# Taking the segment sum's product ahead of the bias products in a graph-network kernel

## Chip, cores and metric

The kernel runs on one core of a Trainium2 chip. Its engines are TensorE (PE in the profile, its weight loads PEld), VectorE (DVE), ScalarE (ACT), GpSimd (POOL) and SyncE (SP). Each takes its own instructions in order; they wait for each other through semaphores, called signals here. The metric is the time of one execution in microseconds of the device (us).

## What is computed

One layer of message passing over a graph of 12,500 nodes and 200,000 edges, all sizes 64 per side. `ssp` is softplus minus log 2. Cut to its core:

```python
nodes = node_state[edges].reshape(num_edges, -1)          # rows of source and target, side by side
gates = ssp(edge_state @ We1 + be1) @ We2 + be2
soft_cutoff = 1.0 - jax.nn.sigmoid(5.0 * (edges_distance - (CUTOFF - 1.5)))
gates = gates * soft_cutoff
h = ssp(nodes @ Wn1 + bn1) @ Wn2 + bn2
messages = h * gates
message_sum = jnp.zeros_like(node_state).at[edges[:, 1]].add(messages)
new_state = node_state + (ssp(message_sum @ Ws1 + bs1) @ Ws2 + bs2)
```

The result is the layer norm of `x + new_state`. The edges are sorted by their target node.

## The kernel before

The edges are cut into 391 groups of 512, and the main loop (from L688) has one step for each group. Step i does the first layers of group i+1, the second layers and the message of group i, and the sum of group i-2. The order is written out by hand: the order of the calls in the loop is the order on each engine. Because the edges are sorted, a half group of 256 edges reaches a window of 42 neighbouring nodes, and its sum is a product of its messages with a 0/1 matrix (the one-hot).

TensorE's instructions of a usual step, in order, each with its line:

- `layer1_bias`, L296: the edge layer's bias into the z tile of group i+1 (three rows of bfloat16, 256 columns).
- `layer2_bias`, L347: the second layers' biases into the gh tile of group i (three rows of bfloat16, 512 columns).
- `scatter`, L376: the product of messages and one-hot of group i-2, two matmuls in float32. It writes 84 columns in the second half of the new z tile, where room is left. From twelve steps before the end on (`CLOSE`) it takes the messages of group i-1, those of the step just before. In the first of these steps it takes both.
- `transposes`, L283: the four gathered tiles of group i+1, into the tx tile.
- `layer1_edge`, L301, then a filler, L334 (in the first steps L646, a part of a table), then `layer1_node`, L308, which waits for ScalarE's copy of the transposes, L291.
- a filler, L334, and `layer2`, L354 and L359, which wait for VectorE's L330. Where a node block is due, its products follow: L415, or L443 and L446.

A float32 matmul of the program is two passes in the profile (a transpose is one), so that L376 counts four a step, L359 eight, L354, L308 and L283 four.

ScalarE copies the transposes (L291), copies single columns (L259), and takes exponential and logarithm of the z tile (L322, L325). VectorE multiplies the second layer's result with the cutoff (L368, which waits for L359) and makes the message (L372), then the softplus (L330) and the one-hot (L277), and adds the sums' product to the running sums (L396, after the logarithms).

GpSimd issues the gathers, L204: four indirect DMAs a group, of 128 rows of x each. Some groups have three, where one tile comes by single columns instead. The gathered tiles `xg` have eight buffers, and the last reader of one is the group's `scatter`. So GpSimd may run ahead until it meets a buffer whose `scatter` has not been done, and waits there. SyncE issues the loads (L216, L224), which wait for a `scatter` as well.

The z tile has two buffers of two banks, gh and tx have two buffers of one bank.

Of the kernel before, what the change touches and what calls it, by code (L numbers as in the profile page):

```python
# [27 lines left out]
HE = 256  # L28
GE = 2 * HE
W = 42  # L30
# [25 lines left out]
def node_blocks(N):  # L56

    first = N % NB
    assert N > NB and first % 2 == 0 and first <= HE
    sizes = ([first] if first else []) + [NB] * (N // NB)  # L60
    return [(sum(sizes[:i]), n) for i, n in enumerate(sizes)]


def block_steps(N, NG):

    steps = []
    for at, n in node_blocks(N):
        share = sqrt(min(1.0, (at + n) / N))
        spread = sqrt(share * (1.0 - share) / (NG * GE))
        steps.append(ceil(NG * (share + SPREADS * spread)))  # L70
    return steps
# [33 lines left out]
def gnn_resnorm_kernel(ctx: ExitStack, tc: tile.TileContext, a: dict, out: bass.AP, E: int):  # L105
# [24 lines left out]
    def z_tile():  # L130
        return psum.tile([P, 2, NB], F32, name="z")
# [46 lines left out]
    def note(key, ins):  # L178
        made.setdefault(key, []).append(ins)
        return ins  # L180

    def behind(ins, *keys):

        for key in keys:
            for other in made.get(key, []):
                tc.add_manual_dep(ins.ins, other.ins.name,
                                  mybir.DependencyInfo(mybir.DependencyClass.Sync, mybir.DependencyReason.DATA),
                                  reason="one place of a step takes its waits")
# [85 lines left out]
    xTs, zs, us, ss, ghs, hs, msgs, scs = ({} for _ in range(8))  # L274

    def onehot(g):
        last = nc.vector.tensor_tensor(xgs[g][:, :, D:DW], iota, rel[:, g, :].to_broadcast([P, K, W]), OP.is_equal)  # L277
        note(("onehot", g), last)

    def transposes(g, *needs):  # L280
        tx = tx_tile()[:DW].rearrange("f (k e) -> f k e", k=K)
        for k in range(K):
            ins = nc.tensor.transpose(tx[:, k, :], xgs[g][:, k, :DW], ident)  # L283
            if k == 0:
                behind(ins, *needs)
        note(("transposes", g), ins)
        xTs[g] = tx
# [4 lines left out]
        xTs[g] = xT.rearrange("f (t h) e -> f h t e", h=2)  # L292

    def layer1_bias(g, *needs):
        zs[g] = z_tile()
        first = nc.tensor.matmul(zs[g][:, 0, :HE], be3.rearrange("q h d -> q (h d)"), ones3, start=True, stop=False,  # L296
                                 skip_group_check=True)
        behind(first, *needs)
# [75 lines left out]
    def scatter(g, sc):  # L374
        for t in range(2):
            ins = nc.tensor.matmul(sc, msgs[g][:, 2 * t : 2 * t + 2, :].rearrange("p h f -> p (h f)"),  # L376
                                   xgs[g][:, 2 * t : 2 * t + 2, D:DW], start=t == 0, stop=t == 1, skip_group_check=True)
        note(("scatter", g), ins)
        scs[g] = sc
# [106 lines left out]
    with tc.manual_schedule():  # L486
# [50 lines left out]
        def clear(first, last):  # L537
            nc.vector.memset(sums[:, first * P : WIDE if last == NCH else last * P], 0.0)
# [43 lines left out]
        for i, w in enumerate((we2[:D, 0, :], wn2)):  # L582
            n = w.shape[0]
# [83 lines left out]
        with tc.tile_pool(name="finish", bufs=1) as finish:  # L667
            blocks = list(zip(node_blocks(N), block_steps(N, NG)))
            last = NG - 1
            parts, begun, complete, rest = {}, None, 0, []  # L670

            def at(f, g, *more):
                if 0 <= g < NG:
                    f(g, *more)

            def behind_by(i):
                close = last - CLOSE
                return [g for g in ([i - 2] if i <= close else []) + ([i - 1] if i >= close else []) if g >= 0]

            for g in range(LOADS - 1):  # L680
                load(g)
            for g in range(2):
                onehot(g)
            lowest(1, NR)
            everywhere(1, NR)
            clear(0, CHUNKS)
            highest()
            for i in range(-1, last - 1):  # L688
                now = parts.pop(i, [])
                early = [part for part in now if part.tensor]  # L690
                at(load, i + LOADS)
                if i >= 0:
                    at(gather, i + AHEAD, range(K), [("transposes", i)] if i < BEHIND else ())
                layer1_bias(i + 1)
                at(layer2_bias, i)
                for n, g in enumerate(behind_by(i)):
                    scatter(g, zs[i + 1][:, 1, HE + 2 * n * W : HE + 2 * (n + 1) * W])
                transposes(i + 1, ("load", i + 1), ("gather", i + 1), ("onehot", i + 1))
                xcopy(i + 1)
                columns(i, 1, finish)  # L700
                layer1_edge(i + 1)
                c = chunk_of(i, NCH)
                if c is None:
                    busy_before_node(i + 1)
                else:
                    beside_sums = zs[i + 1][:, 1, HE + 2 * W : HE + 2 * W + P]
                    chunk(c, beside_sums)
                layer1_node(i + 1)
                exps(i + 1)
                logs(i + 1)  # L710
                if c is not None:
                    keep_chunk(c, beside_sums)
                read_columns(i + 1, 1)
                for g in behind_by(i):
                    window(g)
                if c is not None:
                    clear(c, c + 1)
                at(busy_before_layer2, i)
                at(layer2, i)
                for part in early:  # L720
                    part.tensor(tx_tile())
                at(hcut, i)
                at(message, i)
                softplus(i + 1)
                for part in early:
                    part.others()
                at(onehot, i + 3)
                read_columns(i, 0)
                columns(i, 0, finish)
                choose(finish)  # L730
                for part in now:
                    if not part.tensor:
                        part.others()
                for action in beside.get(i, []):
                    action()
                complete = i
                if blocks and complete >= blocks[0][1] - PREPARE and not begun:
                    begun = node_block(*blocks[0][0], finish)
                    begun.pop(0).others()
                if blocks and complete >= blocks[0][1]:  # L740
                    steps = next(steps for steps in BLOCK_STEPS if i + steps[-1] < last - 1)
                    for n, part in zip(steps, begun):
                        parts.setdefault(i + n, []).append(part)
                    rest = begun[len(steps) :]
                    blocks.pop(0)
                    begun = None
            assert len(blocks) == 1 and begun and not parts


            begun.pop(2).others()  # L750
            transposes(last, ("load", last), ("gather", last), ("onehot", last))
            xcopy(last)
            layer1_bias(last)
            layer2_bias(last - 1)
            scatter(last - 2, zs[last][:, 1, HE : HE + 2 * W])
            layer1_edge(last)
            layer1_node(last)
            for some in (edge, node):
                exps(last, some)
                logs(last, some)  # L760
            square, variance, root, scale, store = (part.others for part in rest)
            square()
            window(last - 2)
            for g in range(last - 1, last + 1):
                if g not in window_at:
                    window_bases(g)
            layer2(last - 1)
            layer2_bias(last)
            softplus(last, edge)
            layer2_edge(last)  # L770
            softplus(last, node)
            layer2_node(last)
            hcut(last - 1)
            message(last - 1)
            scatter(last - 1, tx_tile()[:, : 2 * W])
            variance()
            root()
            hcut(last)
            message(last)
            scatter(last, tx_tile()[:, : 2 * W])  # L780
            window(last - 1)
            window(last)
            hidden, clamp = begun.pop(0)
            hidden(gh_tile())
            scale()
            clamp()
            store()
            for part in begun:
                node_part(part)
# [162 lines left out]
```

## Time and profile before

| | us |
|---|---|
| three runs | 2393.62, 2394.47, 2402.24 |
| median | 2394.47 |
| the profiled execution, timed | 2389.88 |
| its span, first to last instruction | 2388.1 |

The mean granted clock of TensorE was 0.981 of full speed. How to read what the prediction quotes:

- The page's second line has the busy time of each engine, its share of the span, and its instructions.
- A group's row has line, engine, operation, tiles (out<-in) and count, then busy time and mean ns of one, then the idle time of the engine just before them and what ended most of it.
- A row of the list of waits is: who waited, for whom, us in total, times, longest.
- A row of the order of time is: start in us from the span's start, duration, engine, line, operation, tiles, shape, how many rows are merged, and in brackets the idle time of the engine before and who ended it.
- The name behind the arrow is inferred: it is the last instruction on that engine that had ended when the signal came, which need not be the one that was waited for.

### The profile page before, as it was taken

What the parts mean: (1) busy time and instruction counts of PE and PEld (TensorE: products, weight loads), DVE (VectorE), ACT (ScalarE), POOL (GpSimd) and SP (SyncE); (2) the same over time, 40 slices, a digit from 0 to 9 for tenths busy, and PEclk for the clock granted to TensorE, in tenths of its full rate; (3) what the DMA queues carried; (4) which work ended last, traced back from release to release, by engine and by line L of the source; (5) the groups of instructions that cost most, each with busy time, mean ns of one, the idle gap of its engine ahead of it and who ended that gap; (6) DMA issues with size and microseconds to landing.
All of it is one profiled execution on the core that took longest, in us unless ns stands there. A gap on an engine that the chain in (4) does not pass through costs nothing.

```text
span 2388.1 us, 48209 instructions
## 1 busy us (share of the span) xinstructions
PE 1970.5 (83%) x12897; PEld 1656.7 (69%) x12897; DVE 1293.9 (54%) x5966; ACT 1511.2 (63%) x7412; POOL 1417.0 (59%) x1497
## 2 busy tenths in 40 slices
PE   6788888888888888888888888888888888888877
PEld 4666677767776776677677667766777767777765
DVE  4355555555555555555555555555555555555544
ACT  3466666666666666666666666666666666666653
POOL 5665665666666666666666666665665666666650
PEclk9799999999999999999999999999999999999988
DMA  6332232322222222222222222222222222222220
GB/s 185 85 91 68 56 75 56 77 61 71 54 57 56 53 59 54 57 56 62 53 59 55 57 58 55 59 59 54 58 58 56 59 57 60 63 57 58 59 50 14
DMA packets 159679, 148.63 MB, mean 62 GB/s; under 512 B 40564, under 2 KB 108949, under 8 KB 159274
## 3 DMA queue, kind: packets, MB, share of 16 engines
q1 hardware_dynamic: 111194, 94.97, 14.4%
q0 software_dynamic: 47776, 49.02, 10.8%
q8 instruction: 109, 1.79, 0.3%
q14 instruction: 166, 1.36, 0.2%
q10 hardware_dynamic: 434, 1.50, 0.2%
HBM read 135.70 MB, written 9.62 MB: 61 GB/s over the span
## 4 chain that ended last, share of the span: by engine, by line
PE 80%; issue 13%; ACT 3%; DVE 2%; another core or an unknown queue 1%; DMA 0%; DVEq 0%; ACTq 0%
PE z L308 18%; PE gh L359 13%; PE z L376 10%; PE tx L283 10%; PE gh L354 7%; PE z L301 6%; PE gh L334 4%; PE gh L347 3%; PE z L296 3%; PE z L334 2%; ACT xT L291 2%; PE tx L415 1%; PE tx L446 1%; PE z L311 1%
## 5 line engine op out<-in xcount | busy, mean ns | idle before, releaser
L204 POOL DMA_INDIRECT xg<-in_x,src_i x1493 | 1416.8, 949 | 919.3 <-PE tx L283 488.8
L308 PE MATMUL z<-xT,wns 106*128 106x256 f32 x1564 | 459.7, 412 | 359.9 <-issue 285.9
L291 ACT COPY xT<-tx 106x512 f32<-106x512 f32 x391 | 229.1, 586 | 779.3 <-PE tx L283 751.1
L259 ACT COPY column<-xh 128x4 uint8 x6016 | 608.7, 193 | 0.0
L308 PEld LDWEIGHTS z<-xT,wns 106*128 106x128 f32 x1564 | 267.8, 193 | 452.4 <-issue 337.7
L368 DVE TENSOR_TENSOR h<-gh,cut 128x256 f32<-128x256 f32 x391 | 165.9, 424 | 747.9 <-PE tx L283 632.2
L359 PE MATMUL gh<-consts,s 128*128 128x64 f32 x3128 | 396.0, 270 | 0.0
L359 PEld LDWEIGHTS gh<-consts,s 128*128 128x128 f32 x3128 | 385.0, 194 | 0.1
L325 ACT ACTIVATE u<-u,one 128x768 f32<-128x768 f32 x392 | 365.8, 933 | 13.4 <-ACT u L322 0.5
L330 DVE SCALAR_TENSOR_TENSOR s<-u,z 128x768 f32<-128x768 f32 x392 | 368.7, 941 | 0.4 <-issue 0.4
L322 ACT ACTIVATE u<-z 128x768 f32<-128x768 f32 x392 | 314.7, 803 | 43.4 <-PE z L308 19.0
L396 DVE TENSOR_TENSOR sums<-sums,z 64x42 f32 x778 | 152.4, 196 | 291.3 <-issue 207.4
L376 PEld LDWEIGHTS z<-xg,msg 128*128 128x128 f32 x1556 | 205.0, 192 | 140.6 <-issue 121.3
L376 PE MATMUL z<-xg,msg 128*128 128x84 f32 x1556 | 265.1, 293 | 15.3 <-DVE msg L372 15.3
L259 DVE COPY column<-xh 128x4 uint8 x2944 | 246.5, 219 | 0.4 <-issue 0.4
L354 PE MATMUL gh<-consts,s 128*128 128x128 f32 x1564 | 243.3, 279 | 1.3 <-DVE s L330 0.8
L283 PE MATMUL tx<-consts,xg 128*106 128x128 f32 x1564 | 238.1, 276 | 0.0
L301 PE MATMUL z<-eT,consts 128*128 128x256 f32 x782 | 237.3, 386 | 0.0
L354 PEld LDWEIGHTS gh<-consts,s 128*128 128x128 f32 x1564 | 210.0, 195 | 2.0 <-DVE s L330 1.1
L283 PEld LDWEIGHTS tx<-consts,xg 128*106 128x106 f32 x1564 | 182.5, 142 | 0.9 <-issue 0.9
L372 DVE TENSOR_TENSOR msg<-gh,h 128x256 f32<-128x256 f32 x391 | 165.8, 424 | 13.4
L334 PEld LDWEIGHTS gh<-consts 128*128 128x128 f32 x778 | 149.5, 195 | 20.5 <-issue 0.3
(109 smaller groups left out, 1456.2 us busy)
## 6 DMA issues: line engine op xcount, KB each, us to landing
eT<-in_eT SPq DMA_DIRECT2D x195, 256.0 KB
xg<-in_x,src_i POOLq DMA_INDIRECT x1493
wns<-table SPq DMA_DIRECT2D x782, 21.0 KB
table<-tb SPq DMA_DIRECT2D x14, 448.0 KB
side<-in_sides SPq DMA_DIRECT2D x70, 64.0 KB
y<-in_x SPq DMA_DIRECT2D x24, 128.0 KB
out<-y SPq DMA_DIRECT2D x24, 128.0 KB
xh<-in_xh SPq DMA_DIRECT2D x2, 781.5 KB
```

The costliest lines, as they stand in the source:

```text
L204: behind(note(("gather", g), nc.gpsimd.indirect_dma_start(out=xg[:, k, :D], out_offset=None, in_=x, in_offset=bass.IndirectOffsetOnAxis(ap ...
L259: copy(column_tiles[slot].bitcast(U8)[:, 4 * r : 4 * r + 4], xh[:, bass.ds(column_at[queue][j] - xh_at, 4)])
L283: ins = nc.tensor.transpose(tx[:, k, :], xgs[g][:, k, :DW], ident)
L301: nc.tensor.matmul(zs[g][:, 0, :HE], we1.rearrange("a h d -> a (h d)"), eTs[g], start=False, stop=True, skip_group_check=True)
L308: nc.tensor.matmul(zn, wns[:, g % REST, h, :], xTs[g][:, h], start=True, stop=not chosen, skip_group_check=True)
L322: nc.scalar.activation(us[g][:, part], z_of(g)[:, part], AF.Exp)
L325: nc.scalar.activation(us[g][:, part], us[g][:, part], AF.Ln, bias=one)
L330: nc.vector.scalar_tensor_tensor(ss[g].rearrange("p i t e -> p (i t e)")[:, part], us[g][:, part], BIG, z_of(g)[:, part], OP.min, OP.max)
L334: nc.tensor.matmul(z, we1.rearrange("a h d -> a (h d)"), ident, start=True, stop=True, skip_group_check=True)
L354: nc.tensor.matmul(v[:, 0, t], ss[g][:, 0, t, :], we2, start=False, stop=False, skip_group_check=True)
L359: nc.tensor.matmul(ghs[g][:, 1, 2 * t + h, :], ss[g][:, 1 + h, t, :], wn2, start=False, stop=h == 1 and t == 1, skip_group_check=True)
L376: ins = nc.tensor.matmul(sc, msgs[g][:, 2 * t : 2 * t + 2, :].rearrange("p h f -> p (h f)"), xgs[g][:, 2 * t : 2 * t + 2, D:DW], start=t = ...
```

## The change

`scatter` goes ahead of both bias products. As it writes into the z tile of group i+1, that tile is now taken in the loop, and `layer1_bias` takes one only where there is none (before the loop's last calls). `zs` is the dictionary of z tiles by group. The code behind the loop, for the last group, is as before.

```diff
     def layer1_bias(g, *needs):
-        zs[g] = z_tile()
+        if g not in zs:
+            zs[g] = z_tile()
...
                     at(gather, i + AHEAD, range(K), [("transposes", i)] if i < BEHIND else ())
+                zs[i + 1] = z_tile()
+                for n, g in enumerate(behind_by(i)):
+                    scatter(g, zs[i + 1][:, 1, HE + 2 * n * W : HE + 2 * (n + 1) * W])
                 layer1_bias(i + 1)
                 at(layer2_bias, i)
-                for n, g in enumerate(behind_by(i)):
-                    scatter(g, zs[i + 1][:, 1, HE + 2 * n * W : HE + 2 * (n + 1) * W])
                 transposes(i + 1, ("load", i + 1), ("gather", i + 1), ("onehot", i + 1))
```

## The prediction

> **What bounds the kernel now.** I read the page first, then the list of waits, then the order of time of three steps, engine by engine. On the page (span, busy time, the gathers' group) TensorE looks like the bound:
>
> ```profile
> span 2388.1 us, 48209 instructions
> PE 1970.5 (83%) x12897; PEld 1656.7 (69%) x12897; DVE 1293.9 (54%) x5966; ACT 1511.2 (63%) x7412; POOL 1417.0 (59%) x1497
> L204 POOL DMA_INDIRECT xg<-in_x,src_i x1493 | 1416.8, 949 | 919.3 <-PE tx L283 488.8
> ...
> L204 POOL DMA_INDIRECT xg<-in_x,src_i x1493: 938/945/1163, 6.7 to 2335.6; - x187
> ```
>
> The last line, from the view of L204 alone, adds when the first and the last gather start. The 391 steps share this span, about 6.1 us each. The list of waits (sum, times, longest) says who is late:
>
> ```profile
> DVE h L368 <- PE tx L283: 632.2, 279, 2.8
> POOL xg L204 <- PE tx L283: 488.8, 342, 7.2
> POOL xg L204 <- PE z L376: 20.0, 9, 3.2
> PE z L376 <- DVE msg L372: 15.3, 10, 4.0
> ```
>
> The first row is odd. L368 needs the second layer, L359, yet what ended its wait is put down to L283, which runs over a microsecond later. The order of time shows why. GpSimd's gathers over four bursts:
>
> ```profile
> 1162.22 0.94 POOL L204 DMA_INDIRECT xg<-in_x,src_i  x1 [1.43 <-PE tx L283]
> ...
> 1164.71 0.94 POOL L204 DMA_INDIRECT xg<-in_x,src_i  x1 [0.30 <-issue]
> 1166.95 0.94 POOL L204 DMA_INDIRECT xg<-in_x,src_i  x1 [1.30 <-PE tx L283]
> ...
> 1170.69 0.94 POOL L204 DMA_INDIRECT xg<-in_x,src_i  x1 [0.30 <-issue]
> 1173.11 0.95 POOL L204 DMA_INDIRECT xg<-in_x,src_i  x1 [1.48 <-PE tx L283]
> ...
> 1176.88 0.95 POOL L204 DMA_INDIRECT xg<-in_x,src_i  x1 [0.30 <-issue]
> 1179.23 0.94 POOL L204 DMA_INDIRECT xg<-in_x,src_i  x1 [1.40 <-PE tx L283]
> ```
>
> TensorE in the same three steps (the first has three gathers; the second four, and a node block's L415; the third four):
>
> ```profile
> 1164.38 0.94 PE L359 MATMUL gh<-consts,s 128*128 128x64 f32 x7
> ...
> 1166.19 0.60 PE L283 MATMUL tx<-consts,xg 128*106 128x128 f32 x4
> ...
> 1169.10 1.00 PE L359 MATMUL gh<-consts,s 128*128 128x64 f32 x8
> 1170.12 1.13 PE L415 MATMUL tx<-sums,consts 128*128 128x256 f32 x4
> ...
> 1171.61 0.68 PE L376 MATMUL z<-xg,msg 128*128 128x84 f32 x4
> ...
> 1175.21 1.00 PE L359 MATMUL gh<-consts,s 128*128 128x64 f32 x8
> ...
> 1176.57 0.68 PE L376 MATMUL z<-xg,msg 128*128 128x84 f32 x4
> 1177.08 0.60 PE L283 MATMUL tx<-consts,xg 128*106 128x128 f32 x4
> 1177.52 0.60 PE L301 MATMUL z<-eT,consts 128*128 128x256 f32 x2
> ```
>
> And those that wait for L359 (VectorE's L368) and L283 (ScalarE's L291):
>
> ```profile
> 1166.64 0.42 DVE L368 TENSOR_TENSOR h<-gh,cut 128x256 f32<-128x256 f32 x1 [1.35 <-PE z L376]
> 1172.74 0.42 DVE L368 TENSOR_TENSOR h<-gh,cut 128x256 f32<-128x256 f32 x1 [2.67 <-PE tx L283]
> 1178.92 0.42 DVE L368 TENSOR_TENSOR h<-gh,cut 128x256 f32<-128x256 f32 x1 [2.50 <-PE tx L283]
> 1179.05 0.59 ACT L291 COPY xT<-tx 106x512 f32<-106x512 f32 x1 [1.19 <-PE tx L283]
> ```
>
> In the third step L359 ends at 1176.21, L376 at 1177.25, L283 at 1177.68. Their three waiters, L368, GpSimd (L376's signal frees the buffer that its next burst fills) and L291, start at 1178.92, 1179.23 and 1179.05: 2.71, 1.98 and 1.37 us later, almost together. TensorE's signals are held back and come as one bunch. When? The burst's last gather ends at 1176.88 + 0.95 = 1177.83, and L368 starts 1.09 us after it. In the second step the distance is 1.11 (1171.63 to 1172.74), in the first 0.99 (1165.65 to 1166.64), though TensorE had ended L359 2.64 and 1.32 us before. So the bunch follows the gathers, not TensorE's work.
>
> This closes a loop: a burst takes 1177.83 − 1173.11 = 4.72, the hold 1.09, GpSimd's next start 0.31, together 6.12, which is 1179.23 − 1173.11. With three gathers it is 1166.95 − 1162.22 = 4.73. The page has 1493 gathers, 71 fewer than 4 × 391, so some 320 × 6.12 + 71 × 4.73 = 2294 us of the 2388 are this loop; the rest is the start and the steps after the last gather. TensorE's order matters where it changes when this bunch comes, or where no gathers run.
>
> **The change part by part.** The two halves of the sums' product (L376, four passes in the rows) go ahead of L296 and L347. Nothing is added or removed, the z tile is only taken earlier, no wait is added in the steps before the closing ones (their messages are two steps old), and no DMA moves. SyncE's loads at L216 and L224 wait for L376's signal as well, and come with it. The order of the signals stays: L359, L376, L283.
>
> *How far do L376 and L283 move?* Two stretches of the trace have the new neighbours: a step without a sums' product, and the last step, where float32 products follow L359 directly:
>
> ```profile
> 35.50 0.28 PE L296 MATMUL z<-ones,be 3*128 3x256 bf16 x1
> 35.62 0.37 PE L347 MATMUL gh<-row,ones 3*128 3x512 bf16 x1
> 35.92 0.65 PE L283 MATMUL tx<-consts,xg 128*106 128x128 f32 x4
> 36.41 0.60 PE L301 MATMUL z<-eT,consts 128*128 128x256 f32 x2
> ...
> 2363.20 1.00 PE L359 MATMUL gh<-consts,s 128*128 128x64 f32 x8
> 2364.04 0.60 PE L283 MATMUL tx<-consts,xg 128*106 128x128 f32 x4
> 2364.57 0.28 PE L296 MATMUL z<-ones,be 3*128 3x256 bf16 x1
> ```
>
> Four float32 passes behind L359 start 0.84 after it and end 0.60 later. So L376 would end 1.44 after L359's start, against 1177.25 − 1175.21 = 2.04 now: 0.60 earlier. Four float32 passes to L296 take 0.53, L296 to L347 0.12, L347 to L283 0.30, L283 to L301 0.49. From L359 to L301 that is 0.84 + 0.53 + 0.12 + 0.30 + 0.49 = 2.28, against 2.31 now. The change of number format is paid once either way; L283 and all behind it stay within 0.03 us.
>
> *A usual step* (some 370 of 391: without the 9 and the 12 below). L376's signal stands behind L359's, which is held until the burst has ended, so being ready 0.60 earlier buys nothing: 0 us. The second step above is the check. There L415 puts L376 at 2.51 us behind L359's start, 1.15 later than in the third step, and the loop took 1173.11 − 1166.95 = 6.16 instead of 6.12. If 1.15 later costs 0.04, 0.60 earlier gains at most about 0.02, × 370 = 7 us. I take 0 and keep −7 for the range.
>
> *Steps in which L376 itself ends GpSimd's wait*: 9 in the list of waits. There the burst starts up to 0.60 earlier: at most 9 × 0.60 = −5.4; two of them belong to the closing steps, where the message sets L376. I take 7 × 0.60 = −4.2.
>
> *The closing steps* (the last twelve) scatter the previous step's message, which VectorE has only just to make:
>
> ```profile
> 2341.82 0.37 PE L347 MATMUL gh<-row,ones 3*128 3x512 bf16 x1
> 2342.74 0.68 PE L376 MATMUL z<-xg,msg 128*128 128x84 f32 x4 [0.55 <-DVE msg L372]
> 2343.26 0.60 PE L283 MATMUL tx<-consts,xg 128*106 128x128 f32 x4
> 2343.69 0.60 PE L301 MATMUL z<-eT,consts 128*128 128x256 f32 x2
> ...
> 2341.81 0.42 DVE L368 TENSOR_TENSOR h<-gh,cut 128x256 f32<-128x256 f32 x1 [0.26 <-PE gh L359]
> ```
>
> L296 and L347 now run under that wait. Afterwards L376 waits first, in order, with both biases, L283 and, behind it, ScalarE's L291 queued up. L376 to L301 becomes 0.53 + 0.12 + 0.30 + 0.49 = 1.44 instead of 0.95: +0.49 in each of the 10 steps that wait, +4.9 at most. While gathers still run the loop covers it; I take four uncovered steps, +2.0. (Here, after 2335.6, no gather runs, and L368 starts as soon as L359 ends: the hold belongs to the gathers.)
>
> Sum: 0 − 4.2 + 2.0 = −2.2 us on the profiled 2389.88 (span 2388.1 and 1.8 around it). That execution lies 4.6 under the median of the three runs, 2394.47; against the median the forecast is 2392.
>
> **Rivals.**
> *TensorE is truly late* (faster). The page says that matmul ends are modelled. If L376 really ended just before GpSimd's start, it would now end 0.60 earlier and take the loop along: 320 × 0.60 = 192 us, 2202. For it: L368 waits on L359's line alone. Against: L368 and L291 start 0.13 apart though the products lie 1.47 apart; the L415 step is not 1.15 longer; and the distance to the last gather holds. [...] Chance 0.07.
>
> *The bunch comes one signal at a time, and L376's now merges with L359's* (faster). Two signals span 0.13 us, so one is worth about 0.065: 320 × 0.065 = 21, 2371. For it: L376 is finished far ahead of the bunch. Against: it was finished before, too. Chance 0.13.
>
> *The format change in front of L283 costs more than the early rows show* (slower). In the usual step the transposes' weights are the gathered rows; if their load can't start behind L347 as quickly as at 35.92, L283 ends later. With four gathers 1.37 us of slack hide it; with three there is none (L283 ends at 1166.79, and L308 hangs on it). It decides from the first nanosecond in the 71 steps of three gathers. Priced at L347 to L283 once more, 0.30: 71 × 0.30 = +21, 2414. Against: such a step is mostly followed by one with slack. Chance 0.12.
>
> That the order does not change is no rival: it is written out by hand.
>
> **How the numbers follow.** Forecast 0.68, rivals 0.07, 0.13 and 0.12. A measurement can tell 0.5%, 12 us, from no change: 2382 to 2406 is the same. Faster 0.20, same 0.68, slower 0.12. The forecast's own range is 2383 to 2400 (−7 − 1 below, +4.9 and the runs' spread above). With the second and third rival the range is 2371 to 2414; the first stays out.
>
> **What would show it.** In the changed profile L376 follows 0.84 behind L359's start and L283 stays 1.8 to 1.9 behind it; L368, L291 and GpSimd still start within 0.4 us of each other, about 1.1 after a burst; bursts of four still come each 6.1 us; GpSimd's waits ended by L376 shrink; in the closing steps L296 stands behind L376's wait. I am wrong if the interval of the bursts moves by more than 0.04 us.

## The result, and the profile after

| | before | after |
|---|---|---|
| median of 20 runs each, us | 2394.89 | 2403.52 |
| lowest and highest | 2390.25, 2402.24 | 2394.96, 2413.78 |
| ratio, 95% interval | | 1.0032 [1.002, 1.0044] |
| profiled execution, timed (span) | 2389.88 (2388.1) | 2404.8 (2403.0) |
| mean granted clock of TensorE | 0.981 | 0.956 |

The changed kernel is 8.6 us slower, where 2.2 us faster was forecast. That lies inside the 0.5% that counted as no change and inside the range with the rivals (2371 to 2414), but above the forecast's own range (2383 to 2400), and the sign is wrong: the interval of the ratio, from twenty runs of each, leaves out 1. In the changed file, lines from L296 on have moved down by one: the sums' product is now L377, the biases L297 and L348, the second layer L360, VectorE's reader of it L369 and the message L373; L283 and L291 stay.

The page of the changed kernel (span, busy times, granted clock in 40 slices in tenths, the gathers' group):

```profile
span 2403.0 us, 48209 instructions
PE 2022.6 (84%) x12897; PEld 1699.4 (71%) x12897; DVE 1296.6 (54%) x5966; ACT 1512.8 (63%) x7412; POOL 1412.8 (59%) x1497
PEclk8798999999999999999999999999998999999988
L204 POOL DMA_INDIRECT xg<-in_x,src_i x1493 | 1412.6, 946 | 933.0 <-PE tx L283 438.5
```

The instructions are the same, 12897 on TensorE, yet they were busy for 2022.6 us instead of 1970.5. Only TensorE's time has grown; VectorE, ScalarE and GpSimd were busy as long as before, to within 5 us. The same products took longer, so the place to look is the clock (0.956 against 0.981).

A usual step in the order of time, first TensorE, then those that wait for it:

```profile
1156.61 1.00 PE L360 MATMUL gh<-consts,s 128*128 128x64 f32 x8
1157.45 0.63 PE L377 MATMUL z<-xg,msg 128*128 128x84 f32 x4
1158.01 0.28 PE L297 MATMUL z<-ones,be 3*128 3x256 bf16 x1
1158.13 0.37 PE L348 MATMUL gh<-row,ones 3*128 3x512 bf16 x1
1158.44 0.65 PE L283 MATMUL tx<-consts,xg 128*106 128x128 f32 x4
1158.92 0.60 PE L302 MATMUL z<-eT,consts 128*128 128x256 f32 x2
1159.36 0.38 PE L335 MATMUL z<-consts 128*128 128x128 f32 x2
1161.07 1.72 PE L309 MATMUL z<-xT,wns 106*128 106x256 f32 x4 [1.33 <-issue]
```

```profile
1154.50 0.94 POOL L204 DMA_INDIRECT xg<-in_x,src_i  x1 [1.48 <-PE tx L283]
...
1158.24 0.94 POOL L204 DMA_INDIRECT xg<-in_x,src_i  x1 [0.30 <-issue]
1160.59 0.94 POOL L204 DMA_INDIRECT xg<-in_x,src_i  x1 [1.41 <-PE tx L283]
...
1166.75 0.94 POOL L204 DMA_INDIRECT xg<-in_x,src_i  x1 [1.47 <-PE z L377]
```

```profile
1160.30 0.42 DVE L369 TENSOR_TENSOR h<-gh,cut 128x256 f32<-128x256 f32 x1 [2.71 <-PE tx L283]
...
1160.43 0.59 ACT L291 COPY xT<-tx 106x512 f32<-106x512 f32 x1 [2.32 <-PE tx L283]
1160.59 0.94 POOL L204 DMA_INDIRECT xg<-in_x,src_i  x1 [1.41 <-PE tx L283]
```

The reader sees three things. The products stand where they were forecast: L377 0.84 behind L360's start, L283 1.83. The loop of the gathers is untouched: the burst ends at 1158.24 + 0.94 = 1159.18, the bunch of signals follows 1.12 later (1160.30), its three waiters start within 0.29 us, and bursts begin 6.09 and 6.16 apart. And L309, 1.13 us long at full clock (at 1154.98, a step earlier), takes 1.72 here: TensorE has fallen to half clock behind 1.33 us without work. The records of the granted clock hold 1.0 and 0.5 alone (40 spans of each here, 13 of each before) and put this half clock at 1161.47 to 1164.89. All changes of the clock in the records of the two kernels lie on a grid of 3.41 us, to within 0.01, and a span of it at half clock is called a half-clock stretch below. Still the next burst comes 6.16 behind the last one: here the loop hides the slow stretch.

Now the twelve closing steps (the last of them stands behind the loop and is unchanged). TensorE in three of them, in the changed kernel:

```profile
2339.43 1.00 PE L360 MATMUL gh<-consts,s 128*128 128x64 f32 x8
2341.41 0.67 PE L377 MATMUL z<-xg,msg 128*128 128x84 f32 x4 [0.97 <-DVE msg L373]
...
2342.44 1.09 PE L283 MATMUL tx<-consts,xg 128*106 128x128 f32 x4
2343.32 1.06 PE L302 MATMUL z<-eT,consts 128*128 128x256 f32 x2
...
2346.78 1.00 PE L360 MATMUL gh<-consts,s 128*128 128x64 f32 x8
2348.76 0.68 PE L377 MATMUL z<-xg,msg 128*128 128x84 f32 x4 [0.98 <-DVE msg L373]
...
2352.75 1.00 PE L360 MATMUL gh<-consts,s 128*128 128x64 f32 x8
```

and in the kernel before:

```profile
2352.14 1.00 PE L359 MATMUL gh<-consts,s 128*128 128x64 f32 x8
...
2354.11 0.68 PE L376 MATMUL z<-xg,msg 128*128 128x84 f32 x4 [0.55 <-DVE msg L372]
...
2357.54 1.00 PE L359 MATMUL gh<-consts,s 128*128 128x64 f32 x8
```

Such a step took 5.40 us (2352.14 to 2357.54). It now takes 5.97 at full clock (2346.78 to 2352.75), and 7.35 where a half-clock stretch falls into it (2339.43 to 2346.78: L302 takes 1.06 instead of 0.60). The message comes no earlier, so the wait has grown from 0.55 to 0.97, and the biases that filled it come afterwards.

The whole span by stretches. The first four rows are the usual steps, the fifth the closing steps; the cuts are the ends of the second layer's product of steps 10, 100, 200, 300, 377 and 389. Columns: window, length, busy time of PE, PEld, DVE, ACT and POOL with instructions, granted clock, share of the DMA engines, GB/s. First the kernel before, then the changed one:

```profile
113.10:647.10 534.00, 443.47 (x2924) 374.39 (x2925) 294.27 (x1417) 352.88 (x1799) 326.34 (x345) 0.98 0.29 69
647.10:1234.90 587.80, 489.18 (x3279) 413.21 (x3279) 320.20 (x1516) 383.11 (x1924) 360.68 (x381) 1.00 0.24 57
1234.90:1828.50 593.60, 498.17 (x3313) 419.42 (x3312) 329.51 (x1548) 389.08 (x1939) 362.35 (x383) 1.00 0.24 57
1828.50:2285.20 456.70, 388.56 (x2566) 326.53 (x2566) 260.88 (x1212) 303.53 (x1504) 278.50 (x294) 0.99 0.25 59
2285.20:2368.50 83.30, 67.34 (x407) 56.23 (x405) 36.10 (x100) 39.50 (x143) 25.81 (x28) 0.92 0.12 28
```

```profile
114.50:650.10 535.60, 460.04 (x2925) 387.22 (x2924) 295.19 (x1416) 352.70 (x1797) 323.80 (x343) 0.95 0.27 68
650.10:1239.50 589.40, 501.79 (x3280) 423.35 (x3278) 320.80 (x1514) 383.73 (x1924) 359.32 (x381) 0.98 0.23 57
1239.50:1835.50 596.00, 502.57 (x3315) 423.63 (x3314) 329.94 (x1549) 389.06 (x1939) 360.92 (x383) 0.99 0.23 57
1835.50:2294.60 459.10, 395.33 (x2566) 333.19 (x2566) 261.46 (x1212) 303.81 (x1504) 277.29 (x294) 0.97 0.23 59
2294.60:2385.00 90.40, 76.25 (x407) 62.65 (x406) 36.13 (x100) 39.75 (x143) 25.51 (x28) 0.83 0.10 25
```

The clock falls everywhere, but the lengths differ: the usual stretches grew by 1.6 to 2.4 us each, 8.0 in 2172 together, the closing stretch by 7.1 in 83. Of the 8.0, 7.7 lie at two places, steps 269 to 276 and 299 to 306: there ScalarE's copy of the transposes waits once for 7.4 and once for 5.8 us while GpSimd issues eight gathers in a row. What makes these two stalls is open. The one near step 302 stands in profiles of the old order too; the one near step 274 lasts longest in profiles of the new order, but not in all of them.

The two profiled executions lie 14.9 us apart, 6 more than the medians; the profile of before is a quick run. Single profiles also differ between executions: with the old order there, the usual steps took 2172.1 us in the kernel before and 2181.2 in run e4_close_only below. So small differences there are read from the ratios only, the closing steps from the rows.

### The profile page after: what moved, and what is told of

It is laid out like the page before. It is cut to its first block, busy times and chain, and to the rows that moved or that the text cites. A ratio compares the mean times of both kernels' runs of the same rounds, so it can differ in the third digit from the quotient of the medians.

```text
span 2403.0 us, 48209 instructions
## 1 busy us (share of the span) xinstructions
PE 2022.6 (84%) x12897; PEld 1699.4 (71%) x12897; DVE 1296.6 (54%) x5966; ACT 1512.8 (63%) x7412; POOL 1412.8 (59%) x1497
## 4 chain that ended last, share of the span: by engine, by line
PE 82%; issue 10%; ACT 4%; DVE 2%; another core or an unknown queue 1%; DMA 0%; DVEq 0%; ACTq 0%
PE z L309 19%; PE gh L360 14%; PE tx L283 13%; PE gh L355 8%; PE z L377 7%; PE z L302 5%; PE gh L335 4%; PE gh L348 3%; PE z L297 3%; ACT xT L291 3%; PE z L335 2%; PE tx L416 1%; PE z L312 1%; PE tx L447 1%
## 5 line engine op out<-in xcount | busy, mean ns | idle before, releaser
L309 PE MATMUL z<-xT,wns 106*128 106x256 f32 x1564 | 485.0, 431 | 331.2 <-issue 223.0
L291 ACT COPY xT<-tx 106x512 f32<-106x512 f32 x391 | 228.7, 585 | 769.4 <-PE tx L283 727.1
L309 PEld LDWEIGHTS z<-xT,wns 106*128 106x128 f32 x1564 | 280.8, 202 | 425.8 <-issue 258.4
L369 DVE TENSOR_TENSOR h<-gh,cut 128x256 f32<-128x256 f32 x391 | 166.0, 425 | 701.7 <-PE tx L283 560.0
L360 PE MATMUL gh<-consts,s 128*128 128x64 f32 x3128 | 402.5, 273 | 0.0
L360 PEld LDWEIGHTS gh<-consts,s 128*128 128x128 f32 x3128 | 393.9, 197 | 0.1
L283 PE MATMUL tx<-consts,xg 128*106 128x128 f32 x1564 | 258.0, 288 | 0.0
L377 PE MATMUL z<-xg,msg 128*128 128x84 f32 x1556 | 245.0, 280 | 14.1 <-DVE msg L373 14.0
L355 PE MATMUL gh<-consts,s 128*128 128x128 f32 x1564 | 254.8, 288 | 0.9 <-DVE s L331 0.8
L283 PEld LDWEIGHTS tx<-consts,xg 128*106 128x106 f32 x1564 | 159.5, 133 | 126.0 <-issue 111.4
L302 PE MATMUL z<-eT,consts 128*128 128x256 f32 x782 | 239.6, 389 | 0.0
L355 PEld LDWEIGHTS gh<-consts,s 128*128 128x128 f32 x1564 | 222.2, 205 | 1.6 <-DVE s L331 1.1
L377 PEld LDWEIGHTS z<-xg,msg 128*128 128x128 f32 x1556 | 209.6, 194 | 17.8 <-DVE msg L373 16.6
L335 PEld LDWEIGHTS gh<-consts 128*128 128x128 f32 x778 | 157.7, 205 | 23.2
L373 DVE TENSOR_TENSOR msg<-gh,h 128x256 f32<-128x256 f32 x391 | 165.9, 424 | 13.4
```

What stands on the lines that cost most here:

```text
L302: nc.tensor.matmul(zs[g][:, 0, :HE], we1.rearrange("a h d -> a (h d)"), eTs[g], start=False, stop=True, skip_group_check=True)
L309: nc.tensor.matmul(zn, wns[:, g % REST, h, :], xTs[g][:, h], start=True, stop=not chosen, skip_group_check=True)
L335: nc.tensor.matmul(z, we1.rearrange("a h d -> a (h d)"), ident, start=True, stop=True, skip_group_check=True)
L355: nc.tensor.matmul(v[:, 0, t], ss[g][:, 0, t, :], we2, start=False, stop=False, skip_group_check=True)
L360: nc.tensor.matmul(ghs[g][:, 1, 2 * t + h, :], ss[g][:, 1 + h, t, :], wn2, start=False, stop=h == 1 and t == 1, skip_group_check=True)
```

## Experiments

Three explanations stood at the start, A, B and C in the expectations. A, the clock: the new order leaves TensorE with poorer stretches in the usual steps (31 with less than 1.70 us of float32 products between 100 and 2280 us, 3 before), half clock sets in (36 stretches of 3.41 us between steps 10 and 377, 8 before), and that costs the time. Where the expectations speak of a gate, that is an estimate of mine: the records show the granted clock and the products that ran ahead of half clock (last section), not what sets it. B, the closing steps: there the biases are now exposed behind the wait for the message. C is the third rival of the prediction, the change of number format ahead of the transposes. Ratios are to the kernel before, on the same chip. Counts of half-clock stretches are from one profile each and scatter: the same usual steps gave 36, 35 and 49 with the new order, 8 and 18 with the old.

**More work for TensorE in the usual steps.** One more filler product a step:

```diff
                 c = chunk_of(i, NCH)
+                busy_before_node(i + 1)
                 if c is None:
```

> The changed kernel with one more filler product (as L335, 128 columns, its result never read) ahead of the first layer's node product in every step. Theory A (clock gate: with the bias products of three rows standing together ahead of the idle wait, some stretches of 3.4 us hold too little float32 work, the clock halves, and a few of these slow steps aren't caught up): the filler adds 0.22 us of work to every such stretch, the mean granted clock goes from 0.956 to 0.975 or more, and the time from 2403 to about 2398 (the closing steps' loss remains). Theory B (the whole loss sits in the closing steps, where the biases no longer run under the message's wait): the clock may rise, the time stays at 2403. Theory C (the change of number format in front of the transposes costs time in steps of three gathers): 2403 or more.

Measured: 1.0017 [1.0006, 1.0027], median 2398.52 us, clock 0.977, as A expected. Of the 36 half-clock stretches 10 are left, the closing steps took 92.9 us. About half of the loss stays though the usual steps are nearly free of half clock; the interval overlaps that of the changed kernel.

The same filler in the kernel before gives its own price:

> The order of before, with one more pair of filler products (L334) ahead of L308 in every step. Theory (clock gate: TensorE falls to half clock after a stretch of 3.41 us that holds too little float32 work, and in usual steps the loop of the gathers absorbs nearly all of it): hardly any half-clock stretch left between steps 10 and 377 (8 in the profile of before), mean clock 0.98 or more, the time 2390 to 2394, since only isolated stretches go. Rival (the filler stands in the way of L308 in the steps of three gathers, where L308 ends the chain): 71 steps times the 0.35 us of a pair at most, 2395 to 2419.

Measured: 1.0015 [1.0005, 1.0025], 5 half-clock stretches. The gain that was expected didn't come: the filler costs more than fewer half-clock stretches are worth here, some 3.6 us on balance. If it costs as much in the changed kernel, most of what was left there is its price. So these two runs alone don't split the loss.

**The filler of before taken out:**

```diff
                 c = chunk_of(i, NCH)
-                if c is None:
-                    busy_before_node(i + 1)
-                else:
+                if c is not None:
```

> The order of before, without the filler products (L334) ahead of L308 (a filler's output is used nowhere). Theory (clock gate): the poorest stretches of 3.41 us fall from 1.75 to some 1.5 us of float32 work, so half clock becomes frequent in the usual steps, mean clock 0.93 or less; double stretches, which the loop does not absorb, appear, and the time is 2405 or more. Rival (the clock does not matter in the usual steps, since the gathers' loop covers TensorE there): the clock falls but the time stays at 2392 to 2397. Rival (the clock depends on something else than TensorE's own work): clock 0.98 and 2394.

Measured: 1.0118 [1.0102, 1.0135], mean clock 0.945 where 0.93 or less was expected, 57 half-clock stretches in the usual steps. The view by stretches, second and fifth row:

```profile
647.40:1241.90 594.50, 491.02 (x3079) 395.17 (x3079) 321.74 (x1515) 384.47 (x1924) 361.40 (x381) 0.96 0.25 56
...
2313.20:2394.90 81.70, 67.38 (x386) 53.88 (x385) 36.12 (x100) 39.65 (x143) 25.90 (x28) 0.87 0.12 29
```

Less work on TensorE, and 28 us more: it did 200 passes fewer than before in the second row (3079 against 3279), and was busy longer. So half clock in the usual steps seems to cost time when there is enough of it: if all 28 us are put down to the 49 further stretches, 0.57 us each. That is no fixed price: at 0.57 the 27 further stretches of the next run, with the new order in the usual steps, would cost 15 us, and it is no slower than before.

**New order in the usual steps alone, and in the closing steps alone.** In both the call of `scatter` stands in two places, under a condition; for the first:

```diff
-                for n, g in enumerate(behind_by(i)):
-                    scatter(g, zs[i + 1][:, 1, HE + 2 * n * W : HE + 2 * (n + 1) * W])
+                def sum_up():
+                    for n, g in enumerate(behind_by(i)):
+                        scatter(g, zs[i + 1][:, 1, HE + 2 * n * W : HE + 2 * (n + 1) * W])
+                if i < last - CLOSE:
+                    sum_up()
                 layer1_bias(i + 1)
                 at(layer2_bias, i)
+                if i >= last - CLOSE:
+                    sum_up()
```

> The new order in the usual steps alone; the closing steps in the old order. Theory A: clock about 0.96, the usual steps' share of the loss remains: 2398 to 2400. Theory B: all of the loss is gone, 2395 or, with my forecast's gain in steps where L377 ends GpSimd's wait, 2391. Theory C: 2403.

> The old order in the usual steps, the new one in the twelve closing steps alone. Theory A: clock about 0.98, only the closing steps' loss: 2398 to 2400. Theory B: 2403. Theory C: 2395.

Measured: usual steps alone 0.9996 [0.998, 1.0012], closing steps alone 1.0046 [1.0029, 1.0062], medians 2393.57 and 2405.92 us, nearest to what B expected. The closing stretch of the first and of the second:

```profile
2288.10:2372.80 84.70, 68.77 (x407) 57.63 (x406) 36.13 (x100) 39.72 (x143) 25.79 (x28) 0.90 0.12 27
```

```profile
2292.60:2383.20 90.60, 75.57 (x407) 61.59 (x407) 36.15 (x100) 39.77 (x143) 25.70 (x28) 0.83 0.11 26
```

That settles the place. The new order costs 11 us (7 to 15) when it stands in the closing steps alone, and nothing that can be measured in all the others (−5 to +3), though those had as many half-clock stretches as the changed kernel (35). The profiles of the two runs lie 11.7 us apart: 5.9 are the closing stretch, 0.7 the usual steps, and 3.8 the first steps, up to step 10. Those took between 107.4 and 114.5 us in the thirteen profiles, with the old order and the new alike, so 6 to 7 us is what the rows bear out.

**What in the closing steps?** More filler under the wait, two pairs in the 0.97 us for which TensorE has nothing to do:

```diff
                 zs[i + 1] = z_tile()
+                if i > last - CLOSE:
+                    busy_before_node(i + 1)
+                    busy_before_node(i + 1)
                 for n, g in enumerate(behind_by(i)):
```

> The changed kernel, with two more pairs of filler products (0.88 us at full clock) ahead of the sums' product in the closing steps, where TensorE waits about 0.97 us for the message. Theory (the closing loss has two parts: the bias products that now run behind that wait, and the half clock that this brings): steps 380 to 388 all take 5.97 us without half clock, in place of 64.2 us together 54 to 57, and the closing stretch 90.4 falls to 84 to 87; the time is 3 to 6 us below the changed kernel's, a ratio to before of 1.001 to 1.002. Rival (the exposed bias products alone make the loss, and the clock is hidden): the closing stretch stays at 90 and the ratio at 1.003. Rival (the fillers delay the sums' product): steps above 5.97 at full clock.

Measured: 1.0012 [0.9999, 1.0025]. TensorE in two closing steps:

```profile
2372.31 1.00 PE L360 MATMUL gh<-consts,s 128*128 128x64 f32 x8
2373.15 0.66 PE L335 MATMUL z<-consts 128*128 128x128 f32 x4
2374.29 0.68 PE L377 MATMUL z<-xg,msg 128*128 128x84 f32 x4 [0.48 <-DVE msg L373]
...
2378.29 1.00 PE L360 MATMUL gh<-consts,s 128*128 128x64 f32 x8
```

The fillers don't delay the sums' product (L377 is 1.98 behind L360, as without them), and the steps from 384 to 388 run at 5.97 to 6.19 with no half clock. In steps 381 and 383 it stayed, two stretches each. Steps 380 to 388 took 63.3 us where 54 to 57 were expected, and the closing stretch 89.5 where 84 to 87 were: the profile, of the slowest of the twelve runs, missed both and is nearer to the rival's 90. The ratio is as expected, and its interval leaves out the rival's 1.003.

Both fillers together:

> The changed kernel with the additional filler in every step and those of the closing steps together. Theory (usual steps gain about 4 us where the sums' product ended GpSimd's wait, the closing steps lose about 4 through the exposed bias products, and the rest of the loss was the clock): both fillers add up, the ratio to before is 0.999 to 1.001. Rival (there is a loss beside these two): 1.002 or more.

Measured: 1.0009 [0.9999, 1.0019], as expected; 10 half-clock stretches in the usual steps, one in steps 380 to 388. The closing stretch:

```profile
2291.40:2377.40 86.00, 74.15 (x469) 63.55 (x468) 36.14 (x100) 39.58 (x143) 25.56 (x28) 0.92 0.12 27
```

Here the clock is that of before (0.92), so what is left is the exposure. From the starts of the second layer's products, steps 380 to 388 took 56.6 us before, 59.6 here, 64.2 in the changed kernel, with one, one and six half-clock stretches. That gives 3.0 us to the exposed biases and 4.6 to the five further stretches. These are single profiles; in two others with the old order there (e3_usual_only, e5_before_filler2) the nine steps took 58.1 and 58.2 us, with two stretches each. Steadier are the last five, 384 to 388, in which at most one gather starts: 27.8 to 27.9 us in the four profiles with the old order there and three-row biases, 30.4 and 30.6 with the new order and the fillers, none of these with half clock, and 32.9 in the changed kernel with two stretches. So the exposure is 0.5 us a step, and half clock comes on top of it.

**Biases on 128 rows.** The bias operands have three rows in use. Here they have 128, with zeros in 125; the result of the products is the same:

```diff
-    ones3 = const.tile([PIECES, HE], BF16, name="ones3")
-    be3 = const.tile([PIECES, 2, D], BF16, name="be3")
+    ones3 = const.tile([P, HE], BF16, name="ones3")
+    be3 = const.tile([P, 2, D], BF16, name="be3")
...
+        for padded_rows in (be3, row3, rs3):
+            nc.vector.memset(padded_rows, 0.0)
...
-            nc.vector.tensor_copy(be3[:, k, :], ps[:, 0, :])
+            nc.vector.tensor_copy(be3[:PIECES, k, :], ps[:, 0, :])
```

First in the changed kernel, then in the kernel before, then with the new order in the usual steps alone:

> The changed kernel with the bias operands on 128 rows instead of 3 (the other rows are zeros), so that the bias products keep their place, length and result but use all rows of TensorE. Theory A, if what the gate counts is rows in use: half-clock stretches nearly vanish, mean clock 0.975 or more, time about 2397 to 2399. If it counts the data's switching, nothing changes. Theories B and C: clock and time stay, 2403.

> The order of before, with the bias operands (ones3, be3, row3, rs3) on 128 rows, 125 of them zeros, instead of 3. Theory (the gate weighs a product by the rows in use, so the bias products now count as work): clock 0.98 or more, and since before has few half-clock stretches, the gain is small: 2386 to 2391. Rival (the full rows gain otherwise too, for instance by a cheaper change of number format or by the weight loads): the same -20 us that they gave on the changed kernel less its closing loss, 2383 or less, with the rows L296, L347, L283 standing closer together.

> The new order in the usual steps, the old order in the twelve closing steps, and the bias operands on 128 rows. Theory (the closing order costs 7 to 8 us, the half clock in usual steps 5 or so, the new order's own gain is 4): the best of all, 2375 to 2381, below the 2383 of full rows with the new order everywhere. Rival (full rows already take away the closing steps' loss, since the half clock made it): 2382 to 2384, the same as full rows with the new order everywhere.

Measured: 0.9956 [0.9942, 0.9969], 0.9966 [0.9953, 0.9979] and 0.9946 [0.9931, 0.9962]. All three beat both kernels; the last is 13 us faster than before, as expected. The first two gained more than was expected of the clock (2383.38 us against 2397 to 2399 in the changed kernel, 2381.49 against 2386 to 2391 in the kernel before), and the clock is not the whole reason: in the second the granted clock was 0.973, below that of before, with 24 half-clock stretches in the usual steps against 8. TensorE in a usual step of the second:

```profile
1154.44 1.00 PE L359 MATMUL gh<-consts,s 128*128 128x64 f32 x8
1155.28 0.27 PE L296 MATMUL z<-ones,be 128*128 128x256 bf16 x1
1155.39 0.38 PE L347 MATMUL gh<-row,ones 128*128 128x512 bf16 x1
1155.61 0.57 PE L376 MATMUL z<-xg,msg 128*128 128x84 f32 x4
1156.01 0.60 PE L283 MATMUL tx<-consts,xg 128*106 128x128 f32 x4
1156.45 0.60 PE L301 MATMUL z<-eT,consts 128*128 128x256 f32 x2
```

L301 starts 2.01 behind L359 instead of 2.31, with the same products between and more rows in the biases alone (L359 to L296 takes 0.84 instead of 0.93, L347 to L376 0.22 instead of 0.30, L376 to L283 0.40 instead of 0.52; before, from 1152.07): what I had put down to the change of number format goes in good part with the rows in use. This helps where TensorE ends the chain. Seven bursts of three gathers with a node block in their step took 5.40 us each to the next burst before (mean) and 5.00 here, 2.8 us together; where the rest of the 8 us comes from is open.

A last try, one filler pair under the wait of the closing steps of the best kernel:

> The kernel of the last batch with the new order in the usual steps, the old order in the closing steps and full rows, with one more pair of filler products (0.44 us) ahead of the sums' product in the closing steps, where it waits about 0.55 us. Theory: the half clock in steps 381 and 383 goes, uncovered steps stay at 5.40 to 5.66, closing stretch 79 to 82; the time is 0 to 4 us below the 2376.6 of that kernel, a ratio to before of 0.993 to 0.995. Rival (those two stretches come from the waits of the node blocks, not from this one): no difference.

Measured: 0.9959 [0.9945, 0.9973], no gain; half clock stands in steps 381 and 383, one stretch each, so filling this wait doesn't remove it. The forecast of 0.993 to 0.995 was missed, the rival came out.

## Why the prediction was right and wrong

*The loop and the hold: right.* Plain bursts of four were 6.133 us apart before and 6.143 after (medians of 258 and 255), those of three 4.736 and 4.742. That is far below the 0.04 at which I would have been wrong. TensorE's order by itself did not matter here where the gathers set the pace.

*L376 and L283: right.* L377 stands 0.84 behind L360, L283 1.83, L302 2.31, against forecasts of 0.84, 1.8 to 1.9 and 2.28.

*Steps in which L376 ends GpSimd's wait, −4.2: the size came out, at other steps than those counted, so in part by luck.* The seven bursts of three gathers with a node block fell from 5.40 us to 4.85 in the mean, −3.9 together (−2.5 with the usual steps alone changed). But of the nine waits that I counted from the list only two belong to these seven (the gathers that start at 1592.5 and 1688.6 us); three of the others stand at bursts of eight gathers or behind half clock, two at bursts of four, two in the closing steps. With 128 rows, new order against old in the usual steps is 0.9946 against 0.9966, −4.8 us; the intervals overlap, and the seven make 1.0 of it in the profiles. And I said that the waits ended by L376 would shrink. They grew from 20.0 us in 9:

```profile
DVE h L369 <- PE tx L283: 560.0, 259, 2.8
POOL xg L204 <- PE tx L283: 438.5, 303, 3.8
POOL xg L204 <- PE z L377: 80.9, 48, 6.9
PE z L377 <- DVE msg L373: 14.0, 10, 3.0
```

The name is the last instruction that had ended when the signal came. At 1166.75 above, behind a half-clock stretch, the signal came at 1166.49 and L283 ended at 1167.05, too late to be that; L377 is named in its place, in a burst of the usual length. A half-clock stretch reaches into the last 4 us before the gather in 26 of the 48; for the other 22 I have no such reading. With both fillers the row is 25.1 us in 14. A row of this list was read as a fact about the wait after I had shown myself that its names are inferred.

*The usual steps at 0: right as a sum only.* With usual steps alone changed the ratio is 0.9996. A gain of some 3 to 4 us at the seven bursts is in it, and something gives it back; that this is the half clock is argued from e6_before_nofiller, not shown, and the two stalls of the changed kernel's profile are a rival. The prediction has no clock in it; the sentence "buys nothing: 0 us" looked at the loop and not at what the order does to TensorE's own speed.

*The closing steps: the step that failed.* The prediction put it as "+4.9 at most. While gathers still run the loop covers it; I take four uncovered steps, +2.0". Measured: the nine steps from 380 to 388 are 7.6 us longer together (381 and 383 are shorter, the other seven longer). The price of a step was right, 0.5 us where no half clock falls into it. Exposure at equal clock is +3.0, inside my bound but above my choice, since more than four steps were uncovered. The +4.9 was no bound: five half-clock stretches, which the sum put at nothing, added +4.6, more than the exposure. The mechanism (biases queue behind the message) was right, its place was right, its size was not: +7.1 in the profile and 11 (7 to 15) by the run with the closing steps alone. With a filler under the wait the loss shrinks from 0.32% to 0.12%, 4.8 us; the intervals overlap, so this alone proves little, but the size fits those 4.6 us.

So the sum reads: about −4 from the seven bursts, +7 to +11 from the closing steps, and the rest of the +8.6, some +2 to +6, from the usual steps. That last term is a remainder, and the ratios bound it only to a few us.

*The rivals.* None came: the bunch did not come earlier (2202 and 2371), and L348 to L283 is still 0.31, so 2414 is not the reason either, though the time lies on its side.

## What to carry to other kernels

Here half clock followed 129 of 148 stretches of 3.41 us with less than 1.70 us of float32 products (three-row biases). So when products are reordered, work out the load per stretch too, not only the order: in the usual steps, where the gathers set the pace, 27 further slow stretches cost nothing that could be measured (0.9996); in the closing steps, where TensorE ends the chain, five cost 4.6 us. Before moving a product that waits ahead of products that don't, list what used to fill that wait. And where few products have few rows in use, try them padded to all rows: here zeros in 125 rows gained 8 us in the kernel before and 18 in the changed one (0.9956 against 1.0032).

## What the runs showed of the hardware

**Half clock behind gaps of 1 to 2 us.** In the changed kernel half clock set in at 29 places between steps 10 and 377. At 27 of them the longest gap between TensorE's products that reaches into the 3.41 us before was 1.06 to 1.94 us (1.33 us ahead of L309 above), so TensorE had not stood still for a whole stretch of the grid; the other two lie in the two stalls, in gaps of 7.39 and 5.52 us.

**Half clock and the rows in use.** For each 3.41 us stretch at full clock between 100 and 2280 us I added up the time of float32 products (from start to next start, at most 0.26 us each, 0.33 for the 256 columns of L301 and L308) without the biases. In the nine profiles with three-row biases 148 stretches had less than 1.70 us, half of the stretch, and 129 of them were followed by half clock (before 3 of 3, changed kernel 27 of 31, without filler 23 of 23); of those above 1.80 us only 24 of 5274. In the four profiles with 128 rows 194 stretches had less than 1.70 us of float32, and only 24 were followed by half clock. With the bias products counted too, 30 stretches of these four are left below 1.70 us, and 24 of them were followed by half clock. So the two groups agree (129 of 148, 24 of 30) when bias products of three rows are left out of the sum and those of 128 rows are in it. This is a reading of the traces; no run measured a product alone.

**Clock and time go together within a kernel.** Over the 20 runs of the changed kernel the mean granted clock went from 0.948 to 0.964, and 0.01 of it was worth 10 us (correlation −0.78). Between kernels it isn't a measure of the time: with the usual steps alone changed the clock was 0.965 in the profile, 0.016 below before, and the time the same. The time depends on where the slow stretches fall: the 27 further ones in those usual steps cost nothing that could be measured, five in the closing steps 4.6 us.
